# Graph layer with experts: twenty instead of sixteen first nodes take their edge maximum over all of b, their pauses end earlier, and the last edge slice has 93 steps

## The chip, the cores and the metric

One core of a Trainium2 chip runs the whole layer in one launch. The metric is device microseconds (us) of that core. The core has a matrix engine (PE in the profile, with PEld for its weight loads), a vector engine (DVE), a scalar engine (ACT), GpSimd (POOL), the SyncE queue (SP) and 16 DMA engines. Every engine works through its own instructions in order.

## The reference

There are 3125 nodes with 256 features and 100,000 edges, sorted by destination. The destinations are skewed: node number is 3125 times the square of a uniform number, so node 0 alone has some 1,800 edges and low nodes have far more than high ones.

```python
xn = _layernorm(x)
# gnn: maximum over the edges of a node
e = relu((xn[dst] - xn[src]) @ theta_w.T + theta_b + xn[src] @ phi_w.T + phi_b)
gnn = segment_max(e, dst)            # 0 where a node has no edge
# mix: linear attention over all nodes, 8 heads of 64, k and v normalized
mix = (q @ (k.T @ v) / N) @ w_out.T + b_out
x = x + gnn + mix
# ffn: 8 experts of 256 -> 1024 -> 256 with gelu, each node takes its best two
x = x + sum over the top 2 of weight * (gelu(expert_norm(layernorm(x)) @ W1 + b1) @ W2 + b2)
```

The part of an edge that depends on its source is `b[src]`, with b a matrix of 3125 rows of 256 numbers; the part that depends on the destination is added after the maximum.

## The kernel before

**Edges.** The edges lie in descending order of destination in 782 columns of 128 lanes. A *step* is one column: GpSimd gathers 128 rows of b by an indirect DMA (`gather`, L126, 128 KB), and DVE folds them into a running maximum along the lane (`fold`, L406, one instruction on 128x256). Steps are gathered into windows of up to eight (`wide`, five buffers that are used in turn); when a window is folded, SyncE stores it to `s_d` (`move`, L118), and its buffer is free for a later gather.

**Groups.** Nodes are in 25 tiles of 128. `GROUPS` gives five groups of tiles, from the last tile to tile 0, and `STEPS` the slice of steps that holds each group's edges: 134, 151, 185, 158 and 99, in all 727 steps. The remaining 55 columns (`REST`) are of the lowest nodes only.

**First nodes.** Those 55 columns are never gathered. For the 16 lowest nodes (`FIRST`) the maximum is made another way. `first_nodes` (L1126) counts, for each of these nodes, which of the 3125 sources it has in those columns: for each column DVE makes two one-hot tiles (L1140, 128 wide, and L1142, `FIRST * NT` wide) and PE multiplies them into one PSUM bank. What is absent becomes a very negative number (`absent`). Later `first_maxima` (L1149) goes over b in seven chunks of four tiles (the last has one tile). It turns a chunk (L1181), and then for each first node PE spreads that node's row of `absent` over a bank (L1200, one matmul for each tile of the chunk) and DVE adds it to both halves of the turned chunk and takes the maximum (`seen`, L1165, two instructions of 512 columns with an accumulator read each). One pass for one node and one chunk is called a pass below. At the end the 16 maxima go into the row of node tile 0 (`of_first`, the clock entry `firsts`).

**Routing and experts.** When a group's slice is folded, `group(g)` adds the carried maxima to its tiles (`token_tile`), picks two experts for each node, and `dispatch` works out slots for the nodes (`slots`) in two halves of the group and scatters the rows on GpSimd (L133) to `xs_d`. Then `Stream.go` runs the eight experts over that group's rows in units (L700 first matmul, L702 gelu, L724 second matmul). Group 3 (tiles 1 to 3) stays on chip. The tile of node 0 to 127 is last and takes all eight experts densely (`dense_tile`), with `b2_sb` added by one matmul (L956). After that `combine` gathers the experts' rows and writes the output.

**Order.** The order on PE, DVE, ACT and SyncE is written by a planner inside the program: generators yield a number of ticks, and `tick()` lets the ones that are due emit their instructions between gathers; one gather, scatter or store by GpSimd moves the clock `now` by one. `first_maxima` waits `PACE - 1` ticks or `PACE_TOKENS - 1` ticks a pass, and it stands still while `clock["tokens"]` is in `PAUSES`, that is while group 1 or group 2 is being routed:

```python
                if clock.get("tokens", 0) in PAUSES:
                    ...
                    while clock.get("tokens", 0) in PAUSES:
                        yield 1
```

`group` sets the entry when it begins and removes it when both halves of `dispatch` are done:

```python
        while any(t[2] is one for t in tasks for one in waiting):
            yield 1
        clock.pop("tokens")
```

Of the kernel before, what the change touches and what calls it, by code (L numbers as in the profile page):

```python
# [8 lines left out]
F32 = mybir.dt.float32  # L9
# [15 lines left out]
D = 256  # L25
# [5 lines left out]
E = 8  # L31
# [8 lines left out]


GROUPS = ((17, 25), (10, 17), (4, 10), (1, 4), (0, 1))
STEPS = (134, 151, 185, 158, 99)
CAPS = (256, 256, 256, 128)
PARTS = (2, 2, 2, 1)
ROUND = E * CAPS[0]
# [2 lines left out]
COL = [sum(STEPS[:g]) for g in range(G + 1)]  # L49


FIRST = 16
CHUNK = 4
CHUNKS = -(-NT // CHUNK)
REST = T - COL[G]
# [22 lines left out]
def gps_layer(ctx: ExitStack, tc: tile.TileContext, x, src, dst, thetaT, phiT, biases, wq, wkvT,  # L78
# [142 lines left out]
    thirds = keep.tile([ROWS_3, 2 * D + E], BF16, name="thirds")  # L221
    which_bias = keep.tile([ROWS_3, E + 1], BF16, name="which_bias")
    wr_sb = keep.tile([P, 2, E], F32, name="wr_sb")
    b2_sb = keep.tile([E, D], F32, name="b2_sb")
    sm = keep.tile([P, SM, E], F32, name="sm")
    table = keep.tile([P, 1], F32, name="table")
    of_first = keep.tile([FIRST, D], F32, name="of_first")
# [509 lines left out]
    class Stream:  # L737
# [112 lines left out]
        def go(self):  # L850
            units = Units(self.ps, self.act)
            u, q = 0, -1
            self.next_w(-3)
            start(self.more_w())
            yield 25
            while True:
                if u == len(self.lots):

                    for _ in units.last():
                        yield room()  # L860
                    units.behind = None
                    if u < len(self.lots):
                        continue
                    if not self.open:
                        break
                    if G - 3 in self.through:
                        nc.scalar.activation(table, eps, AF.Sqrt)
                    while u == len(self.lots):
                        yield 1
                if ("xe", u) not in self.held:  # L870
                    self.rows(u // 2)
                    self.hots(u)
                    yield 1.5 if self.on_chip(u) else 8
                    self.turn(u)
                    yield 2
                    self.scaled(u)
                    yield 2
                g, e = self.lots[u]
                v = u // 2
                ys = self.act.tile([P, 2, D], F32, name="ys")  # L880

                def done(r, yp, u=u, ys=ys):
                    g, e = self.lots[u]
                    n = self.half(u)
                    add_bias(yp[0:n, :], e, n, slice(0, D), False, True)
                    nc.scalar.copy(ys[0:n, r, :], yp[0:n, :])  # L886
                    if r == PARTS[g] - 1:
                        at = (g * ROUND if g < G - 2 else 0) + e * CAPS[g]
                        rows = ys_d[g][at:at + CAPS[g]].rearrange("(p s) d -> p s d", p=n)
                        move(nc.scalar, rows, ys[0:n, 0:PARTS[g], :])  # L890
                        if u + 1 == len(self.lots) or self.lots[u + 1][0] != g:
                            self.through.add(g)

                between = {4: lambda: self.turn(u + 1), 6: lambda: self.scaled(u + 1)}
                if self.on_chip(u + 1):
                    between[1] = lambda: self.hots(u + 1)
                elif u % 2 == 0:
                    between[1] = lambda: self.rows(v + 1)
                q += 1
                if q:  # L900
                    between[7] = lambda q=q: (self.next_w(q, self.parts), self.part())
                at_step = dict(between)
                for f in (0, 2, 5):
                    between[f] = lambda f=f: (self.part(), at_step.get(f, int)())
                w1t, w2t = self.weights(q)
                for _ in units.run(e, w1t, self.held["xe", u], w2t, done, between, PARTS[g], self.half(u)):
                    yield room()
                u += 1
            for k in range(3):
                dense_w[DENSE[k]] = self.held["w", self.slot[q][DENSE[k]]]  # L910
                dense_slot.append(self.slot[q][DENSE[k]])
            dense_half(0, 1, xn_hi[:, 7:7 + FC, :].rearrange("p i d -> p (i d)"), nc.scalar)
            clock["through"] = True

# [4 lines left out]
            nc.vector.tensor_scalar(by[:, k, :], pick[:, k, 0, :], share[:, k, i:i + 1], None, op0=OP.mult)  # L919
        nc.vector.tensor_add(full, by[:, 0, :], by[:, 1, :])  # L920

    def dense_tile(act, ps, mm, i, shared, w, next_w, order=range(E), ready=None, homes=None):


        tr = mm.tile([P, 2, P], F32, name="mm")
        for c in range(2):
            nc.tensor.transpose(tr[:, c, :], xn2(i)[:, c * P:(c + 1) * P], ident)
        xT = homes[0].rearrange("p (c k) -> p c k", c=2) if homes else act.tile([P, 2, P], F32, name="xT", bufs=1)
        nc.vector.tensor_copy(xT, tr)
        held = {}  # L930
        yield 1

        def scaled(k):
            if k < E:
                e = order[k]
                held["xe", e] = act.tile([P, 2, ROWS], F32, name="xe")
                for c in range(2):
                    nc.vector.tensor_scalar(held["xe", e][:, c, 0:P], xT[:, c, :], sm[:, c, e:e + 1],
                                            sm[:, 2 + c, e:e + 1], op0=OP.mult, op1=OP.add)

        while ready is not None and "through" not in ready:
            yield 1
        scaled(0)
        o = homes[1] if homes else act.tile([P, D], F32, name="o", bufs=1)

        def second_bias():

            bt_p = mm.tile([E, P], F32, name="mm")
            nc.tensor.transpose(bt_p, full, ident)
            bt = act.tile([E, P], F32, name="bt", bufs=1)  # L950
            nc.vector.tensor_copy(bt, bt_p)
            held["bt"] = bt

        def add_second():
            bb = mm.tile([P, D], F32, name="mm")
            nc.tensor.matmul(bb, held["bt"], b2_sb, start=True, stop=True)  # L956
            nc.vector.tensor_add(x_sb[:, i, :], x_sb[:, i, :], bb)

        units = Units(ps, act, True)
        for k, e in enumerate(order):  # L960
            def done(r, yp, k=k, e=e):
                if k == 0:
                    nc.vector.tensor_scalar(o, yp, full[:, e:e + 1], None, op0=OP.mult)
                else:
                    nc.vector.scalar_tensor_tensor(o, yp, full[:, e:e + 1], o, op0=OP.mult, op1=OP.add)

            between = {1: lambda k=k: scaled(k + 1)}
            if k == 1:
                between.update({3: second_bias, 5: add_second})
            if k > 1:  # L970
                between[1] = lambda k=k: (next_w(k - 2), scaled(k + 1))
            while k == 1 and not shared:
                yield 1
            for _ in units.run(e, w[e][0], held["xe", e], w[e][1], done, between, 1, P):
                yield 1
        nc.vector.tensor_add(o, o, x_sb[:, i, :])
        for _ in units.last():
            yield 1
        n = rows_in(i)
        move(nc.sync, out[i * P:i * P + n, :], o[0:n])  # L980
# [75 lines left out]
    def loads():  # L1056
# [1 line left out]
        of_biases = ea.tile([ROWS_3, 2 * D + E], F32, name="of_biases")  # L1058
        move(nc.scalar, of_biases, biases)
        move(nc.scalar, wr_sb, wr.rearrange("(c p) e -> p c e", p=P))  # L1060
        move(nc.scalar, b2_sb, b2)
        move(nc.scalar, sm, small)
        low = ea.tile([1, D], F32, name="low")
        nc.vector.memset(low, NEG)
# [297 lines left out]
    def group(g):  # L1362
# [14 lines left out]
        if g == G - 1:  # L1377
            shared = []
            dense = dense_tile(at_hand["act"], at_hand["ffp"], mm, 0, shared, dense_w, next_dense,
                               DENSE, clock, [xn_hi[:, CHUNK + 1 + k, :] for k in range(2)])  # L1380
            start(routed_tile(0, last_rows(at_hand["tok"], 0, rows), slices, carried, top[:, 0, :], top_i[:, 0, :],
                              newton=True, then=lambda: start(dense), also=ends, at_once=1))
            while 0 not in routed:
# [14 lines left out]
        for i in range(i0, i1):  # L1398
            start(routed_tile(i, last_rows(at_hand["tok"], i, rows), slices, carried, top[:, i - i0, :],
                              top_i[:, i - i0, :], newton=g == 1, at_once=2 if g > 1 else None))  # L1400
            yield PER_TILE[g]
        while any(t[2] is one for t in tasks for one in waiting):
            yield 1
        clock.pop("tokens")
        if g == 0:
            start(first_maxima())
        if g == 1:
# [25 lines left out]

    dense_w = {}
    dense_slot = []

    def dense_half(e, k, to, queue=nc.sync):

        move(queue, to, w12[e, :, k * HALF:(k + 1) * HALF])
        dense_w.setdefault(e, {})[k] = (first_of, second_of)[k](to)  # L1440
# [176 lines left out]
    with tc.If(wrong > 0), tc.tile_pool(name="general", bufs=1) as ge:  # L1617
# [88 lines left out]
        with tc.tile_pool(name="all", bufs=2) as al, tc.tile_pool(name="all_w", bufs=2) as aw, \  # L1706
                tc.tile_pool(name="all_p", bufs=2, space=PSUM) as ps, \
                tc.tile_pool(name="all_mm", bufs=1, space=PSUM) as pm:
            for i in range(NT):
                top = al.tile([P, 1, E], F32, name="top")  # L1710
                top_i = al.tile([P, 1, E], U32, name="top_i")
# [9 lines left out]
                for e in range(-3, 0):  # L1721
                    next_w(e)
                spread(al, i, made[0])
                all_of(dense_tile(al, ps, pm, i, made, w, next_w))


# [45 lines left out]
```

## Time and profile before

| | |
|---|---|
| median of 6 runs | 1650.66 us (1641.49 to 1654.02) |
| the profiled execution | 1634.64 us, span 1632.8 us |
| mean granted TensorE clock | 0.772 |
| PE busy | 952.3 us (58%), 4275 matmuls |
| DVE busy | 782.2 us (48%), 2511 instructions |
| POOL busy | 845.8 us (52%), 879 instructions |
| ACT busy | 332.1 us (20%), 800 instructions |
| gathers of edges | 727, from 73.7 us to 1480.5 us, 968 ns each on the mean |
| folds of the last slice | 1331.0 to 1497.0 us |

Busy time is the time in which an engine executes; a step of the work can be short of its engine's time while another engine waits. Stretches of the span are told as "745 to 825" in us from its start. A wait that is put down to "remote" or to "another core or an unknown queue" is one whose releaser the profile doesn't show; there is one core only.

### The profile page before, as it was taken

The page shows a single profiled execution, that of the slowest core. Times are in us where ns is not written, and L with a number is a line of the kernel's source. Part 1 is how long each engine was busy: PE and PEld are TensorE (multiplying, and loading weights), DVE is VectorE, ACT ScalarE, POOL GpSimd, SP SyncE. Part 2 cuts the span into 40 slices and gives each one's busy share as a digit, 9 for nine tenths or more (in the row PEclk, how much of TensorE's full clock was granted, in tenths as well). Part 3 has the DMA queues.
Part 4 walks back from the last instruction along what each step waited for, and adds up shares of the span by engine and source line. Part 5 has one row for each costly group of instructions (what it writes and reads, how often), then busy time and mean ns, then how long its engine had stood idle before and what let it go on. Part 6 is the DMA issues. An engine that isn't in the chain of part 4 may idle for free.

```text
span 1632.8 us, 14460 instructions
## 1 busy us (share of the span) xinstructions
PE 952.3 (58%) x4275; PEld 711.1 (44%) x4275; DVE 782.2 (48%) x2511; ACT 332.1 (20%) x800; POOL 845.8 (52%) x879
## 2 busy tenths in 40 slices
PE   3513774644444157467578777641376937369767
PEld 2401332322222146356446555431265725268657
DVE  3556984644338135355166545355355714624323
ACT  1300221210112012122122222320122302123222
POOL 6174465466665745634646443537655374732361
PEclk7756997876766569778889788775698968579879
DMA  7442564557545528555446675435458753549373
GB/s 224 137 127 90 193 221 140 193 174 291 212 158 216 179 96 281 168 179 206 142 168 201 239 252 198 150 113 201 138 205 289 268 168 118 208 138 337 125 258 116
DMA packets 102662, 306.84 MB, mean 188 GB/s; under 512 B 20259, under 2 KB 44186, under 8 KB 91694
## 3 DMA queue, kind: packets, MB, share of 16 engines
q0 software_dynamic: 42400, 115.28, 22.9%
q1 hardware_dynamic: 29164, 109.58, 17.3%
q10 hardware_dynamic: 31010, 80.97, 14.7%
q8 instruction: 36, 0.59, 0.1%
q14 instruction: 52, 0.43, 0.1%
HBM read 184.99 MB, written 120.75 MB: 187 GB/s over the span
## 4 chain that ended last, share of the span: by engine, by line
PE 39%; another core or an unknown queue 27%; issue 13%; DVE 12%; ACT 5%; DMA 2%; POOL 1%; ACTq 0%; POOLq 0%; SPq 0%; DVEq 0%
PE hp L700 14%; PE yp L724 11%; DVE g L406 3%; PE v L1234 2%; ACT ring L702 2%; PE mm L1200 1%; PE trf L453 1%; PE bp L281 1%; PE k L1234 1%; PE mm L453 1%; DMA g<-b_d,srcI 1%; PE mm L499 1%; POOL xs_d L133 1%; DVE tiles L1142 1%
## 5 line engine op out<-in xcount | busy, mean ns | idle before, releaser
L126 POOL DMA_INDIRECT g<-b_d,srcI x727 | 703.8, 968 | 500.3 <-issue 214.2
L406 DVE SCALAR_TENSOR_TENSOR g<-g,cut 128x256 f32<-128x256 f32 x722 | 349.0, 483 | 97.4 <-remote 34.5
L702 ACT ACTIVATE ring<-hp,sm 128x256 f32<-128x256 f32 (+1 forms) x320 | 136.4, 431 | 633.3 <-remote 287.1
L1165 DVE CUSTOM_DVE_ANT_0 xn_hi<-bT,mm 128x512 bf16<-128x512 f32 (+1 forms) x224 | 140.4, 627 | 260.2 <-PE mm L1200 93.9
L700 PE MATMUL hp<-xe,big 128*128 128x256 f32 (+1 forms) x768 | 194.3, 381 | 115.2 <-issue 64.8
L700 PEld LDWEIGHTS hp<-xe,big 128*128 128x128 f32 x768 | 137.6, 209 | 143.7 <-issue 69.5
L724 PE MATMUL yp<-big,ring 128*128 128x256 f32 x624 | 179.1, 407 | 9.5 <-issue 8.7
L700 PE MATMUL hp<-xe,w 128*128 128x256 f32 (+1 forms) x448 | 119.9, 400 | 98.3 <-issue 57.8
L700 PEld LDWEIGHTS hp<-xe,w 128*128 128x128 f32 x448 | 86.1, 223 | 118.1 <-issue 62.1
L724 PEld LDWEIGHTS yp<-big,ring 128*128 128x128 f32 x624 | 122.2, 207 | 27.7 <-issue 10.0
L724 PE MATMUL yp<-w,ring 128*128 128x256 f32 x368 | 108.9, 413 | 0.0
L724 PEld LDWEIGHTS yp<-w,ring 128*128 128x128 f32 x368 | 73.6, 211 | 11.2 <-issue 0.6
L126 POOL DMA_INDIRECT r<-s_d,end_i x25 | 23.9, 957 | 97.9 <-DMA s_d<-g 34.6
L1200 PE MATMUL mm<-ident_h,absent 128*128 128x128 bf16 x400 | 45.3, 233 | 46.8 <-issue 23.8
L503 DVE TENSOR_SCALAR none<-mm 128x1 f32<-128x1 f32 x25 | 3.9, 156 | 137.3 <-remote 104.7
L1234 PE MATMUL v<-wkv,xn_hi 128*128 128x512 f32 x56 | 32.9, 717 | 54.9 <-ACT big L1239 51.9
L126 POOL DMA_INDIRECT g<-ys_d,from_i x42 | 40.2, 957 | 42.9 <-DMA out<-g 27.8
L1243 DVE TENSOR_REDUCE var<-big 128x16 f32<-128x1024 f32 x25 | 30.4, 1217 | 62.7 <-ACT big L1240 59.1
L1200 PEld LDWEIGHTS <-absent 128*128 128x128 bf16 x400 | 33.7, 106 | 55.8 <-issue 27.4
L815 ACT ACTIVATE xe<-trf,sm 128x256 f32<-128x256 f32 (+1 forms) x64 | 30.7, 534 | 101.1 <-issue 83.6
L133 POOL DMA_INDIRECT xs_d<-xn_hi,slot_i x28 | 29.6, 1056 | 22.5 <-ACT ys L886 7.8
L499 PE MATMUL mm<-cr,oh 128*128 128x257 f32 x114 | 33.2, 422 | 13.5 <-DVE oh L487 10.2
(322 smaller groups left out, 1283.2 us busy)
## 6 DMA issues: line engine op xcount, KB each, us to landing
s_d<-g SPq DMA_DIRECT2D x75, 1024.0 KB
big<-in_w ACTq DMA_DIRECT2D x48, 512.0 KB
w<-in_w ACTq DMA_DIRECT2D x32, 512.0 KB
s_d<-g SPq DMA_DIRECT2D x13, 896.0 KB
g<-b_d,srcI POOLq DMA_INDIRECT x727
big<-in_w ACTq DMA_DIRECT2D x4, 2048.0 KB
xs_d<-zero ACTq DMA_DIRECT2D x24, 256.0 KB
xn_hi<-xs_d ACTq DMA_DIRECT2D x12, 512.0 KB
```

The costliest lines, as they stand in the source:

```text
L126: got = nc.gpsimd.indirect_dma_start(out=to, out_offset=None, in_=table, in_offset=row_index(index))
L133: put.append(nc.gpsimd.indirect_dma_start(out=table, out_offset=row_index(index), in_=of, in_offset=None))
L406: nc.vector.scalar_tensor_tensor(g[:, j, :], last, cut[:, t:t + 1], g[:, j, :], op0=OP.add, op1=OP.max)
L453: nc.tensor.matmul(am, xnT(i, c), am_w[:, c, :], start=False, stop=False)
L499: nc.tensor.matmul(r2, picks[k], carried[g], start=(k == 0), stop=(k == len(slices) - 1))
L700: nc.tensor.matmul(hp[:, 0:n], w1t[:, c, f, :], xe[:, c, 0:n], start=(c == 0), stop=(c == 1))
L702: nc.scalar.activation(hT[f][:, 0:n], hp[:, 0:n], AF.Gelu, bias=sm[:, 4 + f, e:e + 1])
L724: nc.tensor.matmul(yp[r][0:part, :], hT[q][:, r * part:(r + 1) * part], w2t[:, q, :], start=(q == 0), stop=(q == FC - 1 and self.whole))
L815: nc.scalar.activation(xe[:, c, 0:n], self.held["tr", u][:, c, 0:n], AF.Identity, bias=sm[:, 2 + c, e:e + 1], scale=sm[:, c, e:e + 1])
L1165: nc.vector.tensor_tensor_reduce(unread[:, 0:n * P], bT[:, h, 0:n * P], mask_p[:, 0:n * P], 1.0, NEG, op0=OP.add, op1=OP.max, accum_out=mo ...
L1200: nc.tensor.matmul(mask_p[:, i * P:(i + 1) * P], absent[:, at:at + 1].to_broadcast([P, P]), ident_h, start=True, stop=True)
L1234: nc.tensor.matmul(to, xnT(i, c), wkv[:, c, k * INNER:(k + 1) * INNER], start=(c == 0), stop=(c == 1))
```

## The change

`FIRST` goes from 16 to 20 and the last slice from 99 to 93 steps; `REST` becomes 61 columns. `first_nodes` makes 61 pairs of one-hot tiles, the second 500 instead of 400 wide, and `first_maxima` makes 20 instead of 16 passes a chunk. The entry `tokens` is now removed when all tiles of a group are routed, so that the passes go on while its slots and scatters are still being made. The bias `b2` no longer has its own place on chip: it is loaded late into a free row of `xn_hi` by ScalarE's queue, when the last expert unit has been issued. (The general path, which runs only for inputs that don't fit the plan, gets a tile of its own.)

```diff
-STEPS = (134, 151, 185, 158, 99)
+STEPS = (134, 151, 185, 158, 93)
-FIRST = 16
+FIRST = 20
-    b2_sb = keep.tile([E, D], F32, name="b2_sb")
...
                 dense_slot.append(self.slot[q][DENSE[k]])
+            move(nc.scalar, b2_late, b2)
             dense_half(0, 1, xn_hi[:, 7:7 + FC, :].rearrange("p i d -> p (i d)"), nc.scalar)
...
-            nc.tensor.matmul(bb, held["bt"], b2_sb, start=True, stop=True)
+            nc.tensor.matmul(bb, held["bt"], second, start=True, stop=True)
...
         move(nc.scalar, wr_sb, wr.rearrange("(c p) e -> p c e", p=P))
-        move(nc.scalar, b2_sb, b2)
...
             yield PER_TILE[g]
+        while not all(i in routed for i in range(i0, i1)):
+            yield 1
+        clock.pop("tokens")
         while any(t[2] is one for t in tasks for one in waiting):
             yield 1
-        clock.pop("tokens")
         if g == 0:
             start(first_maxima())
...
+    b2_late = xn_hi[0:E, CHUNK, :]
```

More of the change, by code (lines that the diff above doesn't have):

```diff
@@ L920, in spread, with dense_tile @@
         nc.vector.tensor_add(full, by[:, 0, :], by[:, 1, :])
-    def dense_tile(act, ps, mm, i, shared, w, next_w, order=range(E), ready=None, homes=None):
+    def dense_tile(act, ps, mm, i, shared, w, next_w, order=range(E), ready=None, homes=None, second=None):
         tr = mm.tile([P, 2, P], F32, name="mm")
@@ L1379, in group @@
             dense = dense_tile(at_hand["act"], at_hand["ffp"], mm, 0, shared, dense_w, next_dense,
-                               DENSE, clock, [xn_hi[:, CHUNK + 1 + k, :] for k in range(2)])
+                               DENSE, clock, [xn_hi[:, CHUNK + 1 + k, :] for k in range(2)], b2_late)
             start(routed_tile(0, last_rows(at_hand["tok"], 0, rows), slices, carried, top[:, 0, :], top_i[:, 0, :],
@@ L1708, in gps_layer @@
                 tc.tile_pool(name="all_mm", bufs=1, space=PSUM) as pm:
+            second = al.tile([E, D], F32, name="second", bufs=1)
+            nc.sync.dma_start(second, b2)
             for i in range(NT):
@@ L1723, in gps_layer @@
                 spread(al, i, made[0])
-                all_of(dense_tile(al, ps, pm, i, made, w, next_w))
+                all_of(dense_tile(al, ps, pm, i, made, w, next_w, second=second))
 def kernel(x, src, dst, L0_gnn_theta_w, L0_gnn_theta_b, L0_gnn_phi_w, L0_gnn_phi_b, L0_mix_w_qkv,
```

## The prediction, made before the changed kernel ran

> **What bounds the kernel now.** I read the page's chain that ended last, then busy time in stretches of 50 us, then the costs of the groups that the change touches, then the waits of the two pauses, then the end of the program on PE.
>
> ```profile
> PE 39%; another core or an unknown queue 27%; issue 13%; DVE 12%; ACT 5%; DMA 2%; POOL 1%; ACTq 0%; POOLq 0%; SPq 0%; DVEq 0%
> ```
>
> No engine carries the span. PE has 39% of the chain, and 27% is waiting that the profile can't name.
>
> ```profile
> 150.00:200.00 50.00, 36.09 (x119) 18.22 (x119) 47.24 (x163) 7.50 (x16) 20.38 (x22) 0.86 0.49 167
> ...
> 750.00:800.00 50.00, 37.08 (x167) 30.43 (x165) 11.87 (x48) 8.82 (x21) 32.36 (x34) 0.90 0.60 203
> 850.00:900.00 50.00, 43.82 (x213) 32.52 (x212) 30.49 (x82) 13.35 (x35) 31.07 (x32) 0.94 0.57 191
> 1100.00:1150.00 50.00, 8.61 (x47) 6.35 (x46) 25.61 (x95) 2.97 (x5) 35.81 (x37) 0.50 0.50 178
> 1200.00:1250.00 50.00, 43.63 (x250) 36.67 (x249) 34.96 (x95) 14.52 (x33) 28.82 (x30) 1.00 0.81 289
> 1450.00:1500.00 50.00, 47.25 (x325) 42.93 (x324) 27.19 (x75) 19.23 (x54) 11.47 (x12) 0.97 0.82 286
> ```
>
> The columns are stretch, length, busy us and instructions of PE, PEld, DVE, ACT and POOL, granted clock, DMA share, GB/s. Four regimes show. At 150 to 200, where the one-hot tiles are made, DVE is busy 94%: it is the bound. At 750 and at 1100, the stretches in which a group is dispatched and the passes stand still or have just begun again, POOL issues 34 and 37 gathers and scatters, near its most (one starts each 1.25 us at best, 40 in 50 us), and DVE or PE is mostly idle. At 850 and 1200, where passes, folds and expert units alternate, PE does 213 and 250 matmuls and POOL still gets 32 and 30 done. At 1450 PE is busy 94% with the experts of group 3: there PE is the bound.
>
> The groups that the change multiplies (busy us, mean ns of one, idle before):
>
> ```profile
> L1165 DVE CUSTOM_DVE_ANT_0 xn_hi<-bT,mm 128x512 bf16<-128x512 f32 x192 | 131.3, 684 | 235.4 <-PE mm L1200 88.8 <-remote 72.4 <-PE hp L700 51.9
> L1200 PE MATMUL mm<-ident_h,absent 128*128 128x128 bf16 x400 | 45.3, 233 | 46.8 <-issue 23.8 <-DVE most L1165 21.7 <-DVE rank L615 0.8
> L1165 DVE DVE_READ_ACCUMULATOR2_ANT most<- 128x1 f32 x224 | 18.4, 82 | 0.0
> L1142 DVE TENSOR_SCALAR tiles<-column,of_tile 128x400 bf16<-128x400 int16 x55 | 17.7, 323 | 0.0
> L1140 DVE TENSOR_SCALAR lanes<-column,of_lane 128x128 bf16<-128x128 int16 x55 | 13.8, 251 | 1.5 <-remote 0.8 <-PE v L1234 0.5
> ```
>
> **The change part by part.** The sums are made against the profiled execution, 1634.64 us (span 1632.8, 1.8 us around it). It lies 16.0 us under the median of 1650.66, and I add those 16.0 at the end.
>
> *One-hot tiles.* Six more pairs: the second tile grows from 400 to 500 columns; from the two rows a column costs (323 - 251) / (400 - 128) = 0.265 ns, so it takes 350 ns, and a pair 601 ns: 3.6 us. The 55 old ones grow by 26 ns each: 1.5 us. Together 5.1 us on DVE, which is busy 82.9 of the 90 us from 140 to 230, while POOL waits there for its folds (21.4 us in three waits). Nothing hides it: +5, from 0 to +6. The added PE products (351 ns each) run behind DVE.
>
> These tiles are made between gathers. The 31 gathers of 150 to 216 took 1015 ns each on the mean, the 32 of 850 to 900 took 972: 43 ns more, and three or four gathers beside the added 5.1 us make 0.2 us. [...]
>
> *Passes.* Four more passes in each of six full chunks: 24 x 2 x (684 + 82) = 36.8 us of DVE; four in the last chunk, whose instructions take 284 + 82: 2.9 us. PE gets 4 x 25 = 100 matmuls at 45.3 / 400 = 0.113 us: 11.3 us. Where they go is told by the planner's clock, read while both programs are built. The pause of group 1 was ticks 314 to 409 and now ends at 381, that of group 2 was 520 to 593 and now ends at 571. At 2.2 ticks a pass these 28 and 22 ticks hold 12.7 and 10 passes, nearly all the 24. Elsewhere the density stays, and the expert units start within a few ticks of where they did: the first of group 1 at 433 instead of 423, the first of group 2 at 606 and of group 3 at 745 in both.
>
> In time these are 745 to 825 and 1090 to 1175:
>
> ```profile
> DVE xn_hi L1165 <- PE mm L1200: 36.4, 2, 35.5
> ACT ys L886 <- PE mm L1200: 22.2, 1, 22.2
> ACT ring L702 <- remote: 16.5, 2, 9.9
> DVE tot L602 <- remote: 15.2, 1, 15.2
> ...
> POOL xs_d L133 <- ACT ys L886: 7.8, 1, 7.8
> ```
>
> (waiter, releaser, us, times, longest; 745 to 825.) DVE idles 55.3 of the 80 us there, and 43.9 of 85 in the other, against 19.4 and 15.3 us that the passes need. So there is room by sums. But DVE's queue is in order: the `slots` chain of the second half (L602 to L656, 771.1 to 775.0) now gets some three passes in between, 3 x 1.53 = 4.6 us, and POOL's scatters (7.8 us of waiting in the last row) and then all gathers behind them wait for that. In group 2 the same delay is covered by ten gathers that stand before the scatter of 1122 (7.7 us between the end of `slots` at 1114.4 and that scatter). The 14 folds of the first pause, which ran ten in a row at 775 to 780, get nine passes between them, 14 us; DVE's 35.5 us idle wait after 780 covers most of that, except where POOL stands still from 811 to 825 for a fold: I put 4 there. Sum +9. Bounds: below, -15, the wait of L602, if work that is spread better dissolves it; above, +40, every instruction on the path, which is the row's own busy time. I stay near the low half because DVE is idle more than half of both stretches.
>
> The clock was 0.55 of full in 1090 to 1175. There four L1200 matmuls took 0.61 us instead of 0.39 at full clock, so the passes cost PE up to 0.05 us a matmul more, 2 us for 40 of them. [...]
>
> *End of the passes.* They finish at tick 769 instead of 748, so about eleven of the short ones now stand among the first units of group 3, where PE is the bound: 11 x 0.113 = 1.2 us; +1, from 0 to +5 if PE waits for DVE there.
>
> *Six steps fewer.* Six gathers at 1.25 us are 7.5 us of POOL, six folds 2.9 us of DVE. They don't bring the experts of group 3 forward: these start behind the same gather (679) in both orders. They move the chain of node tile 0 (L1492, L414, L499, L541) one expert unit forward in PE's order, so that the last unit now stands behind it:
>
> ```profile
> 1521.41 4.75 PE L1492 MATMUL mm<-g,xn_hi 128*128 128x256 f32 x12
> ...
> 1531.67 0.70 PE L499 MATMUL mm<-cr,oh 128*128 128x257 f32 x2 [0.52 <-DVE cr L432]
> ...
> 1538.24 0.44 PE L541 MATMUL mm<-ident,xt 128*128 128x128 f32 x2 [2.27 <-ACT xt L529]
> ```
>
> PE idled 0.49, 3.41, 1.68, 0.52 and 2.27 us (8.4) between 1509 and 1543. The last unit's matmuls can fill the last two, and some of the others: -4. Bounds: 0 and -10.7, six times the 1.79 us that a step of the last slice took.
>
> *b2.* One early load less (777 ns of ACT's queue at 74), one late one more, before the load of 1543.97 on the same queue, which is 0.3 us later by that. Its reader L956 ran at 1554.5, eleven us after: at nothing. If that cover were gone, PE would wait for the landing of 8 KB; the nearest, the first load of the program, took 2.85 us.
>
> Sum: 5 + 9 + 1 - 4 = +11. In the profile 1634.6 + 11 = 1646; against the median 1650.7 + 11 = 1662.
>
> **The rivals.** *The pauses become like the mixed stretches: faster.* POOL runs of more than 20 us without a pause go with idle engines: from 1103 to 1165 POOL issued with no pause, and PE had only 47 matmuls in 1100 to 1150. At 850 and 1200 runs are about 10 us long, and PE does four to five times that with only 5 to 7 fewer POOL instructions. If passes between folds cut those runs to some 10 us, which is the point from which this decides, the waits of 15.2 and 7.8 us and 14.3 us of POOL's stand go by half (-19), the sum is 5 - 19 + 1 - 4 = -17, and the time 1634. Against it: DVE's order gives folds later, and POOL has no other source of work.
>
> *Hidden: no change.* The passes cost nothing, the tile chain takes -6: 5 + 0 + 1 - 6 = 0, 1651. For it: the idle sums above; against: the in-order `slots`.
>
> *All on the path: much slower.* Each pass has PE wait for DVE and DVE for PE; at 1121 to 1161 eleven L1165 took 40 us. If folds queue behind every pass, the bound of +40 holds: 5 + 40 + 3 = +48, 1699.
>
> **How the numbers follow.** My own case (+3 to +24) gets 0.38, all on the path 0.12, hidden 0.24, the mixed stretches 0.26. Some 0.5% (8.3 us) is what a measurement of this kernel can tell from no change: own case and the last bound count as slower, 0.50, hidden as same, 0.24, the mixed one as faster, 0.26. The range reaches from the faster rival's 1634 to 1688, my case's upper end and half of the way on to the upper bound; outside lie about 0.1 on each side. The slower cases alone would give 1657 to 1699.
>
> **What would show it.** Right: L1140 and L1142 together near 37 us instead of 31.5; L1165 x280 with some 180 us; the first xs_d scatter of group 1's second half 3 to 8 us later than before against the gathers of the same number; the first expert matmul of group 3 10 to 20 us later; from there to the end some 3 us less. Wrong: if POOL's waits in the two pauses are shorter than before, the rival is right; if the stretch from the first expert of group 3 to the end shrinks by over 10 us, the six steps weighed more than I gave them; if L956 waits for `in_b`, the late load is on the path.

## The result, and the profile after

The changed kernel took 1670.55 us (median of 20 runs, 1662.23 to 1686.29), the kernel before 1652.15 (46 runs, 1634.57 to 1684.35): ratio 1.014, 95% interval 1.0115 to 1.0165. (The ratio leaves out runs that lie more than 1.5% above the fastest of the same kernel, so it is not the ratio of the two medians.) In this comparison the changed kernel is slower, by 18 us by the medians and by 23 by the ratio, where +11 was forecast: the side and the range held, the size did not. The profiled execution took 1662.26 us (span 1660.5) against 1634.64 (span 1632.8).

The page of the changed kernel: the chain that ended last, then the groups that the change multiplies.

```profile
PE 40%; another core or an unknown queue 23%; issue 13%; DVE 12%; ACT 4%; DMA 4%; POOL 3%; ACTq 1%; POOLq 0%; SPq 0%; DVEq 0%
```

```profile
L1164 DVE CUSTOM_DVE_ANT_0 xn_hi<-bT,mm 128x512 bf16<-128x512 f32 x240 | 164.1, 684 | 269.8 <-remote 126.6 <-PE mm L1199 75.6 <-issue 34.0
L1199 PE MATMUL mm<-ident_h,absent 128*128 128x128 bf16 x500 | 56.3, 238 | 71.4 <-remote 29.4 <-issue 19.1 <-DVE most L1164 7.0
L1164 DVE DVE_READ_ACCUMULATOR2_ANT most<- 128x1 f32 x280 | 23.0, 82 | 0.6 <-issue 0.6
L1141 DVE TENSOR_SCALAR tiles<-column,of_tile 128x500 bf16<-128x500 int16 x61 | 21.6, 354 | 0.0
L1139 DVE TENSOR_SCALAR lanes<-column,of_lane 128x128 bf16<-128x128 int16 x61 | 15.6, 256 | 0.1
```

(Lines stand one higher than before in this part.) Every busy time came as worked out: the tiles 37.2 us instead of 31.5, the passes 684 and 82 ns a piece. What grew beyond that is idle time ahead of them: 235.4 us before, 269.8 now.

Where the time came in, by the first expert matmul (L700, now L699) of each group, read from the traces (group 4 is node tile 0):

| us | group 0 | 1 | 2 | 3 | tile 0 | span |
|---|---|---|---|---|---|---|
| before | 557.1 | 832.1 | 1156.9 | 1414.1 | 1543.0 | 1632.8 |
| after | 563.6 | 858.2 | 1175.3 | 1447.6 | 1575.5 | 1660.5 |
| difference | 6.5 | 26.1 | 18.4 | 33.5 | 32.5 | 27.7 |

So 6.5 us came with the tiles, 19.6 up to group 1's experts, 7.7 were won back, 15.1 came on the way to group 3, and 5.8 went from there to the end. (This is one execution of each kernel, 27.7 us apart, where the medians are 18.4 apart.) The stretches of 50 us (columns as before the prediction):

```profile
150.00:200.00 50.00, 36.13 (x119) 18.05 (x119) 48.63 (x167) 7.51 (x17) 21.63 (x22) 0.86 0.48 166
750.00:800.00 50.00, 32.18 (x153) 25.00 (x151) 18.68 (x72) 7.04 (x17) 33.44 (x35) 0.83 0.50 176
1100.00:1150.00 50.00, 11.45 (x69) 8.41 (x67) 28.64 (x118) 5.32 (x11) 31.29 (x33) 0.57 0.50 171
1200.00:1250.00 50.00, 33.95 (x187) 28.83 (x188) 29.06 (x80) 10.20 (x23) 16.48 (x18) 0.80 0.46 159
1450.00:1500.00 50.00, 27.33 (x172) 25.06 (x173) 13.76 (x62) 9.13 (x27) 21.07 (x22) 0.70 0.39 129
```

The stretch at 1200, one of the good mixed ones before (250 matmuls, 30 instructions of POOL), does 187 and 18 now. Its waits, 1211 to 1270:

```profile
POOL g L126 <- DVE most L1164: 33.2, 2, 28.6
ACT ring L701 <- PE hp L699: 22.1, 15, 2.1
ACT ring L701 <- issue: 18.4, 1, 18.4
PEld hp L699 <- ACT xe L814: 18.2, 2, 18.0
DVE xn_hi L1164 <- PE mm L1199: 18.1, 5, 14.0
```

and ahead of it ACT and PE in turn, from their timelines:

```profile
1186.93 0.47 ACT L701 ACTIVATE ring<-hp,sm 128x256 f32<-128x256 f32 x1 [5.60 <-remote]
1196.15 0.47 ACT L701 ACTIVATE ring<-hp,sm 128x256 f32<-128x256 f32 x1 [8.75 <-remote]
1215.07 0.47 ACT L701 ACTIVATE ring<-hp,sm 128x256 f32<-128x256 f32 x1 [18.45 <-issue]
```

```profile
1187.45 2.08 PE L699 MATMUL hp<-xe,w 128*128 128x256 f32 x4 [3.97 <-ACT ring L701]
1196.68 2.08 PE L699 MATMUL hp<-xe,w 128*128 128x256 f32 x4 [7.15 <-issue]
1216.05 2.08 PE L699 MATMUL hp<-xe,big 128*128 128x256 f32 x4 [17.30 <-ACT xe L814]
```

PE's four matmuls of 1196.68 were over at 1198.76; ACT, which waits for nothing else, began at 1215.07. From 1173.3 to 1213.4 POOL issued 32 gathers in one run (numbers 550 to 581, counted from 0), with PE busy 35% of it. Then it had no free buffer and stood 28.6 us until DVE, whose folds stand in order with the passes, had folded. Before, gathers 558 to 597 went in runs of 19.8, 9.9, 9.9 and 10.1 us with PE busy from 65 to 100% of each.

### The profile page after: what moved, and what is told of

It reads as the page before. It is cut to its first block, busy times and chain, and to the rows that moved or that the text cites. A ratio compares the mean times of both kernels' runs of the same rounds, so it can differ in the third digit from the quotient of the medians.

```text
span 1660.5 us, 14797 instructions
## 1 busy us (share of the span) xinstructions
PE 966.9 (58%) x4381; PEld 718.4 (43%) x4381; DVE 812.4 (49%) x2629; ACT 334.2 (20%) x802; POOL 841.4 (51%) x873
## 3 DMA queue, kind: packets, MB, share of 16 engines
q10 hardware_dynamic: 31010, 80.97, 14.3%
## 4 chain that ended last, share of the span: by engine, by line
PE 40%; another core or an unknown queue 23%; issue 13%; DVE 12%; ACT 4%; DMA 4%; POOL 3%; ACTq 1%; POOLq 0%; SPq 0%; DVEq 0%
PE hp L699 14%; PE yp L723 11%; DVE g L405 3%; PE v L1233 2%; POOL g L126 1%; PE bp L280 1%; ACT ring L701 1%; PE mm L1199 1%; PE k L1233 1%; DMA g<-b_d,srcI 1%; PE dots_p L1256 1%; PE trf L452 1%; PE mm L498 1%; POOL xs_d L133 1%
## 5 line engine op out<-in xcount | busy, mean ns | idle before, releaser
L405 DVE SCALAR_TENSOR_TENSOR g<-g,cut 128x256 f32<-128x256 f32 x716 | 345.5, 483 | 76.1 <-DMA g<-b_d,srcI 32.7
L1164 DVE CUSTOM_DVE_ANT_0 xn_hi<-bT,mm 128x512 bf16<-128x512 f32 (+1 forms) x280 | 175.5, 627 | 288.8 <-remote 140.7
L699 PE MATMUL hp<-xe,big 128*128 128x256 f32 (+1 forms) x768 | 196.1, 383 | 121.7 <-issue 74.6
L699 PEld LDWEIGHTS hp<-xe,big 128*128 128x128 f32 x768 | 137.9, 210 | 150.2 <-issue 80.8
L699 PE MATMUL hp<-xe,w 128*128 128x256 f32 (+1 forms) x448 | 119.7, 400 | 110.8 <-issue 62.1
L723 PE MATMUL yp<-big,ring 128*128 128x256 f32 x624 | 175.3, 402 | 0.0
L699 PEld LDWEIGHTS hp<-xe,w 128*128 128x128 f32 x448 | 85.1, 221 | 130.7 <-issue 68.2
L1199 PE MATMUL mm<-ident_h,absent 128*128 128x128 bf16 x500 | 56.3, 238 | 71.4 <-remote 29.4
L1199 PEld LDWEIGHTS <-absent 128*128 128x128 bf16 x500 | 42.1, 109 | 87.1 <-issue 24.0
```

Of the source, the lines that this page charges most:

```text
L405: nc.vector.scalar_tensor_tensor(g[:, j, :], last, cut[:, t:t + 1], g[:, j, :], op0=OP.add, op1=OP.max)
L699: nc.tensor.matmul(hp[:, 0:n], w1t[:, c, f, :], xe[:, c, 0:n], start=(c == 0), stop=(c == 1))
L723: nc.tensor.matmul(yp[r][0:part, :], hT[q][:, r * part:(r + 1) * part], w2t[:, q, :], start=(q == 0), stop=(q == FC - 1 and self.whole))
L1164: nc.vector.tensor_tensor_reduce(unread[:, 0:n * P], bT[:, h, 0:n * P], mask_p[:, 0:n * P], 1.0, NEG, op0=OP.add, op1=OP.max, accum_out=mo ...
L1199: nc.tensor.matmul(mask_p[:, i * P:(i + 1) * P], absent[:, at:at + 1].to_broadcast([P, P]), ident_h, start=True, stop=True)
```

## The experiments

Each kernel was timed against the kernel before on the same chip. The first group of them showed something that the prediction had not allowed for: the kernel before took 1176 us instead of 1652. Both levels came back later, each for a whole session on a chip, and one chip showed both (after_again 1177, after_fourth 1638). I call them the long and the short condition. The first comparison, both first profiles and the prediction belong to the long one.

**Parts of the change, short condition.** Edits, against the changed kernel (a_) or the kernel before (b_):

```diff
a_oldpauses, passes_alone: the pop of clock["tokens"] back behind the wait for the dispatch
a_99, passes_alone:  -STEPS = (134, 151, 185, 158, 93)   +STEPS = (134, 151, 185, 158, 99)
a_16:                -FIRST = 20   +FIRST = 16   (the bound tested for the last slice stays 20)
b_earlypauses:       the pop moved ahead of that wait, nothing else
b_93:                -STEPS = (..., 99)   +STEPS = (..., 93)   (bound 20)
a_nopauses:          -PAUSES = (1, 2)   +PAUSES = ()
```

a_oldpauses: 

> The changed kernel with one part undone: the passes stand still until a group's dispatch is done, as before the change. Theory 1 (the 24 added passes are on the path at about their DVE price, and it matters little where they stand): about +20 us over the kernel before, 1665 to 1675, or a little more because the passes now end some 50 planner ticks later, among the experts of group 3. Theory 2 (the earlier end of the pauses is the harm: passes between folds and the dispatch chain turn the phases of POOL and of the other engines): back to 1645 to 1658. Theory 3 (no part has a price of its own; what counts is the time in which PE, DVE and ACT all stand while POOL issues gathers in one long run): no side is foretold, but the difference in time equals the difference in that idle time, within 5 us.

a_99: 

> The changed kernel with one part undone: the last slice keeps 99 steps, so 727 gathers and 55 one-hot columns. Theory 1 (prediction's terms, with the passes at some 20 instead of 9): the one-hot tiles cost 1.5 instead of 5, the -4 of the six steps is gone: 1670 to 1676, within 4 us of the changed kernel. Theory 3: the time follows the idle time in POOL's runs, and may leave that by more than 8 us either way.

a_16: 

> The changed kernel with 16 first nodes: the maxima of nodes 16 to 19 over their last 61 columns are left out, so 24 long passes and 4 short ones fewer; 93 steps, 61 one-hot columns (narrower tiles), earlier end of the pauses and late b2 stay. Theory 1: the loss goes with the passes: 1645 to 1653. Theory 2 (the earlier end of the pauses is the harm): still 1662 to 1672. Theory 3: idle time in POOL's runs falls by what the time falls.

b_earlypauses: 

> The kernel before with one part done alone: its pauses end when a group's tiles are routed; 16 first nodes, 99 steps. Theory 1: some 23 of the passes move forward into the pauses and none is added: within 6 us of the kernel before. Theory 2: slower by 12 to 20 us. The prediction's faster rival (passes between folds break POOL's long runs): 8 to 17 us faster.

after_again: 

> The changed kernel once more, unaltered, because the four runs before this one showed the kernel before at 1176 us instead of 1652, with POOL issuing without a break and without the long handshakes between PE, DVE and ACT that the first profiles show while POOL issues. Theory 3 (the +18 of the first comparison is only longer handshakes in POOL's runs): where the kernel before takes some 1176 us, the changed one costs what its parts cost there, 0 to +3 us, 1176 to 1179 (a_99 with 99 steps had 1177.9, and six gathers fewer take at most 7.5 from that); where the kernel before takes some 1650, again 1.0 to 1.7 per cent more. Theory 1 (a price on the path, whatever the handshakes do): +15 to +20 us in both.

passes_alone: 

> Twenty first nodes alone (with the late b2): 99 steps, pauses until the dispatch is done. If the earlier end of the pauses matters only because twenty nodes need the room (a_oldpauses against after_again: 12 us where the kernel before takes 1176): 8 to 14 us slower than before, since the passes then end after the last folds. If instead the harm of a_oldpauses came from the six steps fewer, which leave less time ahead of node 0: 0 to 4 us slower. Theory 1 (24 passes at a fixed price wherever they stand): the same +3 as a_99, whose passes are as many. Where the kernel before takes some 1650 us and handshakes are long: theory 3, +10 to +25 us.

b_93: 

> The last slice of 93 steps alone: 16 first nodes (the maxima of nodes 16 to 19 over their last 61 columns are left out), pauses until the dispatch is done, early b2. The prediction put -4 on the six steps and +5 on the one-hot tiles, of which six pairs, 3.5, belong to the steps: -0.5. Six gathers at 1.25 us, 7.5 us, if POOL issues without a break up to the end of the folds and the end follows it: 1168 to 1170 where the kernel before takes 1176. Where it takes some 1650: 0 to -11.

a_nopauses: 

> The changed kernel with no pauses at all: the passes go on at four ticks each while the tiles of groups 1 and 2 are routed. If the passes are bound by room ahead of node 0, 1 to 5 us faster than the changed kernel; if they delay the dispatch through DVE's queue, 3 to 12 us slower, with the first scatter of group 2 later than in the changed kernel. Where the kernel before takes some 1650 us, theory 3: slower than the changed kernel, since more instructions take part in the handshakes while POOL issues in one run.

Measured, with the later repeats after_third, a_16_again, a_16_third and b_earlypauses_again:

| kernel | first nodes, steps, pauses | median us | before | ratio, 95% interval |
|---|---|---|---|---|
| after_again | 20, 93, early end | 1177.22 | 1176.27 | 1.0005, 0.9990 to 1.0020 |
| after_third | the same | 1176.28 | 1176.31 | 1.0004, 0.9987 to 1.0021 |
| a_16 | 16, 93, early end | 1169.83 | 1176.08 | 0.9954, 0.9934 to 0.9974 |
| a_16_again | the same | 1170.56 | 1178.08 | 0.9937, 0.9912 to 0.9962 |
| a_16_third | the same | 1169.19 | 1176.31 | 0.9947, 0.9925 to 0.9969 |
| a_99 | 20, 99, early end | 1177.88 | 1176.08 | 1.0027, 1.0009 to 1.0045 |
| b_earlypauses | 16, 99, early end | 1177.20 | 1176.08 | 1.0004, 0.9987 to 1.0022 |
| b_earlypauses_again | the same | 1177.04 | 1178.08 | 0.9991, 0.9973 to 1.0009 |
| b_93 | 16, 93, late end | 1175.25 | 1175.83 | 0.9989, 0.9961 to 1.0017 |
| a_oldpauses | 20, 93, late end | 1187.25 | 1176.08 | 1.0103, 1.0077 to 1.0129 |
| passes_alone | 20, 99, late end | 1186.98 | 1175.83 | 1.0091, 1.0066 to 1.0115 |
| a_nopauses | 20, 93, no pauses | 1178.13 | 1175.83 | 1.0025, 1.0000 to 1.0051 |

Here the parts have prices. The added passes, with their wider one-hot tiles, cost 7 us (after_third against a_16_third on one chip); six steps fewer, with early pauses, give 3 (a_99 to after_again, on two chips and with intervals that meet) to 7 (b_earlypauses to a_16), with late pauses nothing clear of the noise (b_93, where 6 to 8 were expected), and the whole comes to nothing. Theory 1's 20 us are not there. Theory 2 has it the wrong way round: the earlier end alone changes nothing, and without it twenty first nodes cost 8 us (a_99 to passes_alone) to 12 us (after_again to a_oldpauses) more. Why, DVE's timeline shows, first for a_oldpauses, then for after_third:

```profile
1097.68 0.44 DVE L1208 TENSOR_REDUCE ends_of<-most 128x40 f32<-128x280 f32 x1
1098.60 0.41 DVE L1215 COPY of_first<-mm 20x256 f32<-20x256 f32 x1 [0.48 <-PE mm L1212]
...
1099.38 0.41 DVE L492 TENSOR_TENSOR r<-r,of_first 20x256 f32<-20x256 f32 x1
```

```profile
1041.45 0.41 DVE L1215 COPY of_first<-mm 20x256 f32<-20x256 f32 x1
...
1084.14 0.41 DVE L492 TENSOR_TENSOR r<-r,of_first 20x256 f32<-20x256 f32 x1
```

With the old pauses the maxima are ready 0.4 us before node tile 0 takes them: the passes, which end at 1097.6, 32 us behind the last gather, are on the path. With the early end they wait 42 us. passes_alone shows the same (ready 1096.4, used 1096.8) with 99 steps, so it is the passes and not the shorter slice. a_nopauses ends the passes at 944 instead of 1038 us and gains nothing more (neither side of what was expected of it).

**What differs between the conditions.** POOL's row of the 40 slices, in after_third:

```profile
POOL 6577777777777777777777777777777777777361
```

In the short condition POOL issues from 49 to 1068 us almost without a break, and the other engines work beside it. A signal is here the update of a semaphore by which one engine releases another. I summed from the traces, for each instruction of ACT or DVE whose only foreign releasers are engines and one of them PE, the time from the later of PE's last signalling record and its own engine's last end to its start:

| | condition | signals from PE | late in sum, us | longest |
|---|---|---|---|---|
| before | long | 652 | 457 | 18.6 |
| after | long | 666 | 499 | 18.6 |
| b_earlypauses_again | short | 645 | 24 | 0.4 |
| after_third | short | 655 | 23 | 0.4 |

Signals of ACT and DVE are on time in the long condition (before: 1011 of them, 21 us; after: 1031, 26 us). So in the long condition, of the engines' signals, PE's arrive late, and mostly while POOL issues: 390 of the 457 us belong to signals whose record on PE ended within one of POOL's runs, which cover two thirds of that span (ACT's ring, L702: mean 1.5 us within the runs, 0.2 outside). POOL's issuing alone is not enough: in after_third its runs cover 95% of the span, and the signals are on time (23 us in sum).

The measure is a lower bound, for it counts from PE's last record and not from the one that is waited for. For the passes that one is known, their own mask: from the later of its end and DVE's own last end to their start, 112 passes waited 165.7 us in the trace before (at most 20.9), 140 passes 183.3 us after, and 140 passes 1.7 us in after_third.

Nor is it the signals alone. In the long condition PE itself stood 243 us before and 221 after with nothing that the profile shows to wait for (67 and 54 times, some 95% of it within POOL's runs), in after_third 22 us, 4 times. Counted once where they overlap, these stands and the late signals cover 479 us of the trace before and 24 of b_earlypauses_again; the two spans are 458 us apart. That is a sum over the span and no chain of work, and no trace of the kernel before in the short condition was kept. The profile gives PE's ends as modelled ones, so a late signal and a matmul that ended late are not always told apart: in 36 of the 91 waits of over 1 us before, PE had begun further matmuls meanwhile, in the other 55 it had not. What holds PE up, and what puts a session into one condition or the other, is not known; the kernel before showed both unaltered.

**The price of the late signals.** The theory formed on that (4): a pass costs its signal. Two kernels to test it:

```diff
no_masks:  - six lines: a bank for the mask, and PE's matmuls into it (L1199)
           - ... bT[:, h, 0:n * P], mask_p[:, 0:n * P], ...
           + ... bT[:, h, 0:n * P], bT[:, 1 - h, 0:n * P], ...
a_18:      + FIRST = 18, STEPS = (..., 95)
```

no_masks: 

> The changed kernel with the masks left out of the passes: DVE takes each maximum with the other half of the turned chunk in place of PE's mask, so 500 short matmuls and 140 signals from PE to DVE are gone, while DVE does the same 280 instructions of 512 columns. In the trace of the changed kernel that took 1662 the passes started 83.8 us in sum after PE's last record and DVE's own end (104 of them counted), in the trace of the one that took 1172 only 1.6 us. Theory 4 (a pass costs what PE's signal to DVE comes late, 0.6 to 0.8 us, so 28 passes cost 16 to 23; where the signals are not late a pass is hidden): where the kernel before takes some 1650 us, 30 to 80 us faster than the changed kernel; where it takes 1176, 0 to 8 us faster. Theory 1 (the price is DVE's busy time): no more than 5 us faster in both.

a_18: 

> Half of the change: 18 first nodes, 95 steps, so 14 passes and 59 one-hot columns; the rest as in the changed kernel. Theory 4: where the kernel before takes some 1650 us, half of the loss, +6 to +14; where it takes 1176, within 3 us of it. Theory 1: +8 to +10 in both.

These two fell in the long condition. no_masks took 1587.59 (6 runs, 1559.84 to 1609.81), a_18 1627.74 (6 runs, 1619.74 to 1639.13), the kernel before 1639.35 (11 runs, 1604.6 to 1649.2); its scatter was too wide for an interval, so these are medians only. The changed kernel was not timed beside them. Without the masks the time lies 52 us under the kernel before, as theory 4 wants. But half of the change was not slower, rather 12 us faster, and the signals of no_masks, some 570, came late by some 505 us in its trace (of an execution of 1607.18), more in sum than 652 before. Theory 5 was added: the lateness belongs to POOL's runs and not to the number of signals, and an edit moves it by shifting which signals fall into the runs. Its ranges below reach up to 20 or 30 us, so no run here could speak against it, and it stays untested.

a_16_again: 

> a_16 once more (no added passes, the maxima of nodes 16 to 19 over their last 61 columns left out), for a chip on which the kernel before takes some 1640 to 1650 us; where it takes 1176 again, 0.4 to 0.6 per cent faster as before. Theory 4 (the loss is the price of late signals in 28 passes): 0 to 10 us faster than the kernel before on such a chip. Theory 5 (the phases of POOL's runs decide, and any edit moves the time by up to a per cent either way; a_18 was 12 us faster than the kernel before where theory 4 had it slower): anything from -20 to +20.

b_earlypauses_again: 

> The earlier end of the pauses alone once more, for such a chip; where the kernel before takes 1176, no difference again. Theory 4: no passes are added, so within 5 us of the kernel before. Theory 2 (the earlier end is the harm): +12 to +20. Theory 5: anything from -20 to +20.

after_third: 

> The changed kernel once more, beside no_masks_again and a_16_third on the same chip. Where the kernel before takes some 1640 to 1650 us: theory 4, +15 to +25 us over it; theory 5 (phases of POOL's runs), 0 to +30. Where it takes 1176: within 3 us of it.

no_masks_again: 

> The changed kernel without the masks (500 short matmuls and 140 signals from PE to DVE left out, DVE's instructions as many). Theory 4: some 50 to 80 us faster than the changed kernel where the kernel before takes some 1640 to 1650, 0 to 8 us faster where it takes 1176. Theory 1 (the price is DVE's busy time): no more than 5 us faster in both.

a_16_third: 

> The changed kernel with 16 first nodes (maxima of nodes 16 to 19 over their last 61 columns left out). Where the kernel before takes some 1640 to 1650: theory 4, 15 to 25 us under the changed kernel; theory 5, no fixed sign. Where it takes 1176: 6 to 8 us under the changed kernel, as the two runs before.

These fell in the short condition (table above). no_masks_again took 1202.18 there: 1.0242 of the kernel before (1.0213 to 1.0272), 26 us slower than after_third, against all theories. Its gathers, then those of after_third:

```profile
L126 POOL DMA_INDIRECT g<-b_d,srcI x721 | 730.0, 1013 | 223.3 <-issue 188.1 <-DMA g<-b_d,srcI 13.1 <-DVE g L405 10.2
```

```profile
L126 POOL DMA_INDIRECT g<-b_d,srcI x721 | 710.7, 986 | 222.0 <-issue 186.9 <-DMA g<-b_d,srcI 14.0 <-DVE g L405 10.4
```

Sorted by whether an instruction of a pass overlaps them, gathers took 1095 ns in the mean beside a pass (207 of them) and 979 otherwise in no_masks_again, 978 and 989 in after_third; 1119 and 972 in no_masks, 969 and 968 in the changed kernel's first trace. So beside passes with both inputs in SBUF gathers took 116 and 147 ns longer than the others, beside passes with the mask in PSUM 11 ns less and 1 ns more. In all POOL's gathers were busy 19.3 us longer (730.0 against 710.7), where the whole took 26 longer; that they are on the path was not traced, and what makes them longer no run shows.

**The change once more, long condition.**

```diff
a_pace:  -PACE, PACE_TOKENS, PAUSES = 2.2, 4.0, (1, 2)   +PACE, PACE_TOKENS, PAUSES = 1.9, 4.0, (1, 2)
```

after_fourth: 

> The changed kernel beside a_16_fourth and a_pace on one chip. Where the kernel before takes some 1640 to 1650 us: theory 4, +15 to +25 us over it; theory 5 (phases of POOL's runs), 0 to +30. Where it takes 1176: within 3 us of it, for the fourth time.

a_16_fourth: 

> The changed kernel with 16 first nodes (maxima of nodes 16 to 19 over their last 61 columns left out). Where the kernel before takes some 1640 to 1650: theory 4, 15 to 25 us under the changed kernel; theory 5, no fixed sign. Where it takes 1176: 6 to 8 us under the changed kernel.

a_pace: 

> The changed kernel with the passes planned closer, one in 1.9 ticks instead of 2.2 outside of the token stages, so that they end earlier. Where the kernel before takes 1176: if the six steps fewer are lost because the passes reach into the stretch in which PE is the bound, 2 to 6 us faster than the changed kernel, which would be faster than both; if denser passes delay the folds, 0 to 5 us slower. Where it takes some 1650: theory 5, no fixed sign, within 20 us of the changed kernel.

| kernel | median us (range) | ratio to before, 95% interval |
|---|---|---|
| before | 1644.06 (1617.68 to 1663.73) | |
| after_fourth | 1637.91 (1626.06 to 1646.60) | 0.9971, 0.9939 to 1.0002 |
| a_16_fourth | 1639.78 (1619.20 to 1668.93) | 0.9990, 0.9930 to 1.0049 |
| a_pace | 1639.69 (1623.38 to 1648.54) | 0.9953, 0.9911 to 0.9994 |

The unaltered changed kernel, slower by 1.4% in the first comparison, is not slower here, and the two intervals do not meet. Theory 3, which had it 1.0 to 1.7 per cent slower wherever the kernel before takes some 1650, falls. The added passes (after_fourth against a_16_fourth) have no price that this scatter shows, though the passes' waits for their own masks are as long as in the first pair (174.3 us of 140 passes, 160.5 of 112): theory 4 as a price per pass falls. In the traces they do delay the experts of groups 1 and 3 (851.6 against 830.6, and 1430.9 against 1408.7), and most of it is won back each time: group 2 begins at 1158.9 against 1166.9, the spans end at 1642.7 and 1635.2. The long run of POOL is there again at the same gathers (550 to 581, from 1157.0 to 1197.0, then a stand; waits of 1194 to 1253):

```profile
POOL g L126 <- DVE g L405: 33.6, 2, 29.6
DVE xn_hi L1164 <- remote: 30.7, 3, 17.4
```

so that run came in both traces of the changed program, not in one execution alone. a_16_fourth has one of 30.1 us from the same gather on. a_pace has no run over 21 us between 1161 and 1312, and its profiled span is 1626.7, but its median is that of after_fourth. No version was shown faster than both kernels in both conditions.

## Why the prediction was right or wrong

**Read rightly.** The tiles: +5 forecast, 5.7 us more busy time, group 0's experts 6.5 later. The passes' busy time: 39.7 us forecast (36.8 + 2.9), 175.5 + 23.0 - 140.4 - 18.4 = 39.7 measured. The six steps: -4 and "some 3 us less" from group 3's experts to the end; 5.8 less in the first pair; in the short condition six steps were worth 3 to 7 us of the whole time. The late b2: L956 ran at 1591.4 with no wait. The end of the passes: at 1504.9, with their use at 1555.5. Their matmuls took 56.3 / 500 = 0.113 us each, as before, so the low clock of the pauses put nothing on them that the mean shows.

**The step that failed** is the second term, passes in the two former pauses at +9 (with +1 for their end). In the first pair the stretches that hold them gained 19.6 - 7.7 + 15.1 = 27.0. I placed it near the low end "because DVE is idle more than half of both stretches". That idle time was not free room: L1165 stood there for PE, whose signals arrived late (before: 457 us over the span, 390 of them within POOL's runs), and a pass put there waits for one more of them (idle 269.8 instead of 235.4). The 35.5 us wait that the prediction shows, and one of the passes that now stand in that pause, each with the matmuls that made its mask:

```profile
794.47 0.39 PE L1200 MATMUL mm<-ident_h,absent 128*128 128x128 bf16 x4
...
815.71 0.69 DVE L1165 CUSTOM_DVE_ANT_0 xn_hi<-bT,mm 128x512 bf16<-128x512 f32 x1 [35.53 <-PE mm L1200]
```

```profile
784.12 0.39 PE L1199 MATMUL mm<-ident_h,absent 128*128 128x128 bf16 x4
...
802.51 0.69 DVE L1164 CUSTOM_DVE_ANT_0 xn_hi<-bT,mm 128x512 bf16<-128x512 f32 x1 [14.91 <-remote]
```

Before, the pass began 20.9 us behind its mask, and PE, with nothing to wait for that the profile shows, began its matmuls from 796 to 815 one by one, 0.7 to 2.8 us apart. After, the pass began 18.0 us behind its mask, with folds behind it in DVE's order, the first at 803.13; POOL stood from 800.5 to 811.5, by the profile until PE had turned a part of the next chunk (L1180). From 745 to the experts of group 1, 21 passes waited 39.7 us for masks that were done, where 6 had waited 21.1.

The mechanism named, DVE's in-order `slots`, was not it: the chain did stretch, from 3.9 to 6.5 us, but it began 2.9 us earlier, and the second half's first scatter came 10.9 us behind gather 360 after and 12.5 before, not 3 to 8 us later. What came later lies behind the scatters: from that first scatter (775.5, before 775.8) to the experts of group 1 it took 82.7 us instead of 56.3, and the stretch ahead of group 3 got POOL's run of 40 us.

**The rivals.** The faster one needed shorter waits in the pauses. The three that it named did shrink in the first pause, those of 15.2, 7.8 and 14.3 us to 7.2, 6.1 and 11.0, by 13 in sum; but POOL stood 20.8 instead of 13.3 us ahead of the first scatter and 17.9 instead of 6.4 around 840, and the kernel was not faster. So shorter waits of POOL, which the prediction gave as the sign that this rival is right, were no such sign. The total of the rival that is hidden, no change, is what the short condition shows, but not by its terms: there the passes cost 7 us and the steps give 3 to 7. In the later comparison of the long condition the passes showed no price. In medians the +18.4 lies inside my own case (+3 to +24), in the traced pair +27.7 just above it, short of all on the path (+48).

**What stays open.** The size in the long condition: +1.4% in the first comparison and -0.3% in the second, for the same two programs, have intervals apart from each other. Group-by-group delays of 20 us and their recovery are shown; which of them is left at the end was not settled, nor what brings a session into this condition. That the +9 was too low therefore holds for the first comparison alone, and that PE's late signals make the difference of the two totals there is argued and not shown. My +11 lies between the two, which is luck and not a sum that held.

## To carry to other kernels

An idle engine is room only if its waits would end as soon with more work in front of them (here DVE's idle time ahead of the passes went from 235.4 to 269.8 us); read what ended the idle time first, and if it is a signal that came long after its sender's last record, the busy time of what is added does not tell its price. Before trusting a sum of a few microseconds, see the kernel before more than once, in more than one session: its level, its scatter and its bound may be others (here 1176 and 1652 us). Work that is moved off the path stays off only while its end keeps a margin to its reader; here, in the short condition, early pauses made 42 us of margin out of 0.4.

## What the runs showed of the hardware

The same program took 1176 us in some sessions and 1640 to 1652 in others. In the traces of the slower level signals from PE came late, up to 20.9 us behind the mask that a pass waited for, and mostly while POOL issued indirect DMAs (390 of 457 us before); PE stood 243 us before and 221 after with nothing to wait for that the profile shows, against 22 in after_third at the faster level; the signals of ACT and DVE were 0.02 us late in the mean before. PE's ends on record do not show the delay of its signals, 457 us in sum before and 24 in b_earlypauses_again. And gathers beside a DVE pass with two SBUF inputs took 116 ns (no_masks_again) and 147 ns (no_masks) longer than the other gathers of the same trace, beside a pass with one input in PSUM 11 ns less (after_third) and 1 ns more (the changed kernel's first trace).
